# Floors under squared norms inside later operations, one unit's denominators in PSUM, and a new order, in a fused hybrid block

## The chip, the cores and the metric

One Trainium2 chip, one NeuronCore. The program is a single launch over the whole input. The metric is the device time of the launch in microseconds; the kernel before takes 792.27 us (median of 3 runs, 791.22 to 794.27). Engines are named as the profile names them: PE (TensorE matmul), PEld (its weight loads), DVE (VectorE), ACT (ScalarE), POOL (GpSimd), SP (SyncE, which issues most DMAs).

## What is computed

An input of 8 sequences x 512 tokens x 128 features, float32, goes through four residual layers: a delta-rule attention, a mixture of experts, a chunked linear attention, and the same mixture of experts again.

```python
x = L0_attn_a_x                                   # (8, 512, 128)
x = x + attn_a(layernorm(x), Wq, Wk, Wv, Wb, Wo, conv_q, conv_k, conv_v, o_norm_w)
x = x + ffn(layernorm(x), Wg, W1, W2)
x = x + attn_b(layernorm(x), Wq, Wk, Wv, Wo, bo)
x = x + ffn(layernorm(x), Wg, W1, W2)

# attn_a, 16 heads of 8: q, k, v = silu(short causal conv, 4 taps, of x @ W.T)
n = sqrt(sum(q * q));  q = q / max(n, 1e-6)       # the same for k
v_new = (v_t - k_t @ S) * sigmoid(x @ Wb.T)       # one token after the other
S = S + outer(k_t, v_new);  o_t = (q_t * 8 ** -0.5) @ S
o = o * rsqrt(mean(o * o) + 1e-6) * o_norm_w      # then @ Wo.T

# attn_b, 16 heads of 8: phi = elu + 1, causal in chunks of 128
out = (A @ v + phi_q @ S) / (rowsum(A) + phi_q @ z + 1e-5)

# ffn: 8 experts, the best 2 by x @ Wg, weights renormalised, relu, 128 -> 256 -> 128
```

## The kernel before

The 512 tokens are cut in 8 **units** of 64 tokens (of all 8 sequences, so 512 rows each). A unit passes through these parts, whose names appear in the profile's tiles:

- `prepare(c)` (tiles ending in `_a`): loads x, normalises it, transposes it on PE, projects it. For units 0 to 3 the convolution's four taps are folded into the weights (`wc`, made by `weights_of_taps` and kept in the storage of experts 5 to 7, `resident[5..7]`), so q, k and v take 4 matmuls each (`s_pp_a`); for units 4 to 7 DVE applies the taps. ACT applies silu (`y_a`). The results go to DRAM (`scr`) and come back with heads on partitions (`qk`, `vv`).
- Squared norms (`nrm`): for some units by PE over the feature partitions (`norms_of`, `over_heads`, through DRAM as `scn`), for units in `NEAR_NORMS` (5, 6, 7) and for unit 0's keys by ACT and DVE after the round trip (`near_norms`). Both end with a floor of 1e-12 under the squared norm, on POOL in the first, on DVE in the second. `back` then takes the root of the keys' norms (`ri`, in a PSUM bank, `s_near_a` in the profile), inverts it, and builds the factors `W` of four tokens at a time (`substituted`).
- `recurring`: the delta rule, four tokens a step, 16 steps a unit, 128 in all, one after the other. A step is four DVE operations (`pj`, `factors`, `terms`, `st`) and copies on ACT (`values`, `beside`). POOL multiplies states by queries (`po`); for units 0 to 2 PE sums them (`s_po`).
- `ending`: corrects the outputs, normalises them (`s_rms`), where the query's squared norm stands in place of dividing the query, and sends them through DRAM (`sco`) to `oT`.
- `layers` / `of_rows`: output projection (`s_po_a`), then `moe` under the name f, `linear_attention` under b, and `moe` under g. Unit 7 is done in two halves. `moe` routes (`y_pl`: logits, first and second choice by `first_of_largest`, their weights by `relative`), spreads the combined weights through DRAM (`scw`) over all partitions, and `all_experts` runs every expert on rows scaled by their weight: POOL scales (`wt_xsT`), PE multiplies (`s_ph`), ACT applies relu (`hT`), PE multiplies again (`y_py`). For units 0 and 7 expert 0's rows are scaled before a transpose instead (`TURNED`, `TURNED_IN`).
- `attend`, inside `linear_attention`: POOL forms the products of keys and values (`kv`), PE sums them causally (`s_pc_b`), DVE multiplies by the queries and reduces (`qs`, `nd`), adds 1e-5 to the denominators (`dn`), inverts them and scales. For unit 0 the sums are in SBUF (`nd`), for later units in PSUM (`pS`).
- `loading_later_weights`: SP loads the experts' weights, 3 DMAs an expert. Experts 5 to 7 wait until unit 3's projections have read the tap weights lying there.

**The order.** The program text describes parallel streams; a `Weaver` runs them once and so writes down each engine's order of instructions. Each operation has a modelled duration (the function `duration`, and additions by `weaver.took`). Of the streams whose next step can start soonest, the weaver takes the one with the largest priority: what is still behind it in the chain of work (`chains`, from four earlier passes that only plan) plus two tables of constants, `FAVOURED` by part and `OFFSETS` by stream. On the chip each engine runs its instructions in that order and waits on semaphores; the modelled durations have no other effect. Where the weaver expects PE to wait 0.6 us or more, `keep_busy` puts in matmuls on constants (line 1950, tile `busy`), 0.22 us each for seven tenths of the expected gap; they write to a free PSUM bank and compute nothing that is used.

PSUM has eight banks: five general ones (`banks`, tiles `s_...`), two long ones (`y_...`), and one for the recurrence's `factors`.

All engine calls go through one helper, so nearly all of the profile's rows carry its line, 454; they are told apart by tile.

Of the kernel before, what the change touches and what calls it, by code (L numbers as in the profile page):

```python
# [19 lines left out]
P = 128  # L20
# [17 lines left out]
TURNED = 1  # L38
# [8 lines left out]
ADDED_ON_DVE = (4,5,6,7)  # L47
NEAR_NORMS = (5,6,7)
# [5 lines left out]
TURNED_IN = (0,7)  # L54
# [13 lines left out]
PASSES = ()  # L68

FAVOURED = {  # L70
    ("b", 0.0): 1475, ("b", 1.0): -605, ("b", 2.0): 408, ("b", 3.0): -1141, ("b", 4.0): 1159, ("b", 5.0):
    -397, ("b", 6.0): -3095, ("b", 7.0): -2237, ("b", 7.5): -2071, ("beside",): 1509, ("ending",): 696,
    ("f", 0): 1839, ("f", 1): 922, ("f", 2): 673, ("f", 3): -941, ("f", 4): 1648, ("f", 5): 1050, ("f", 6):
    -1587, ("f", 7): 767, ("f", 7.5): -2892, ("g", 0.0): 1576, ("g", 1.0): 901, ("g", 2.0): 357, ("g", 3.0):
    7212, ("g", 4.0): -253, ("g", 5.0): -2424, ("g", 6.0): -246, ("g", 7.0): 1986, ("g", 7.5): -2626,
    ("outputs",): 7, ("prepare", 0): -904, ("prepare", 1): -3306, ("prepare", 2): 224, ("prepare", 3):
    -1571, ("prepare", 4): -839, ("prepare", 5): -16, ("prepare", 6): 680, ("prepare", 7): -2427, ("recur",
    0): 3219, ("recur", 1): -6342, ("recur", 2): -2844, ("recur", 3): 482, ("recur", 4): -2744, ("recur",
    5): -1405, ("recur", 6): 1064, ("recur", 7): -724, ("values",): 149, None: -1498,
# [4 lines left out]
    -5735, -5206, -179, -62, -5753, 0, -6219, -6323, 29, -6838, 1464, 2372, 2338, -2, 1277, -3446, -3136,  # L84
    2417, -3137, -2112, -3119, -3650, -311, 76, 1, 3, -3, 77, -342, -7970, 977, -20, -4091, 3665, -19, 806,
    -4343, -4621, -4648, -4379, 711, 806, -5289, 1734, 1900, 1275, 623, -5269, -420, -380, -832, -1479, 50,
    -758, -790, 125, -3620, 585, -553, 237, 2322, 2064, -5521, 501, -5381, -5928, -3498, -40, 2563, 4086,
    10628, -5495, 782, 11097, 2142, 524, -2998, -175, 1440, -9862, 334, 747, 94, -5047, -6796, 307, 308,
    -1787, -402, -3506, -63, -187, 265, -2927, -6059, -6411, -6618, 0, -4528, -6371, -6553, -6091, -5056,
    263, -538, -1107, -6503, -6983, -6, -6510, -36, -961, -967, 294, 389, -6742, -8230, -142, -7747, -8737,  # L90
    -7250, -7254, -7665, -422, 1935, 282, -996, -6683, -9031, 177, 1221, 466, 360, -7342, 552, -8817, -42,
    -7371, 101, 1699, 247, 245, 186, -7410, 57, 713, -5151, 127, -91, -80, -5933, 56, -6006, -6402, 412,
    -6116, -445, 35, 2434, -4925, -4928, -4874, -938, 1079, 406, -7960, 775, 519, -186, -183, -6551, -7752,
    -7695, -8113, 429, 2079, 1870, 73, 72, 717, 130, -428, -37, 347, 2267, 385, -69, 3340, -640, -367, 165,
    -831, -1483, 0, 486, -5539, -200, -199, -399, -34, 2547, -7582, -106, -2671, 11037, 1388, 1383, 1120,
    -962, 17, -1270, -6162, -175, -5673, 211, 50, -7246, -2444, -7484, -2599, -386, 24, -1456, -1295, -1542,
    449, 95, 3319, -2490, -5181, -17, 250, 1245, 968, 926, -3459, -1, -51, -7241, -6288, -40, -5786, 456, 0,
    2, -7292, 471, -361, -79, -6239, 1121, 209, 228, 171, -490, -335, -1339, -4313, -4533, -173, -162,
    -1885, -4676, -5235, -6460, -342, -6601, -6575, 266, 235, 4646, 4647, 78, -899, -7489, 388, -348, 4,
    2051, 1488, -3366, -170, -1594, -5834, -4738, -590, -6081, 2703, 771, 806, 2101, -1052, -4471, -334,  # L100
    10046, 384, -6869, -6546, 10224, -8058, 323, -1252, 463, 8950, 0, -8361, 1480, -113, -361, -8416, -9767,
    -47, -200, -9523, 27, -8517, -60, 66, -8349, -229, -9575, -9613, 177, 0, -516, 2087, 1808, 1102, -3472,
    -3462, -3444, -261, -48, -604, -199, 8924, -1499, -2626, 0, -5333, -68, 0, -3882, -1964, 1388, 1387,
    -3692, -5022, -5065, -555, 136, 6558, 1420, 1897, 1801, 9994, 299, 277, 324, -41, 8082, 391, 7156, 7157,
    -5841, -322, -1273, -5351, 627, 9366, -2233, -2747, 1391, 674, -7825, -11438, -30, 775, 2023, 1821,
    -1660, -376, -7698, 679, -3112, 1424, -5849, 0, -55, 151, -899, 680, -7529, -8147, 148, 896, 1077, 914,
    339, 108, 425, -1456, -5019, -1472, -477, 2580, -4207, -3854, -4163, -8696, -1145, -4645, -48, -435,
    -49, -441, -2007, 528, -6603, 2721, 2590, 71, 790, 1764, 678, -1104, -11, -8403, -631, -307, -17, 8979,
    -26, 111, 125, -3643, 387, 709, -7661, -6188, -1529, 52, -267, -2256, -1638, -163, -7464, -7718, -7716,
    -1060, 1984, -7251, 341, -416, 74, 246, 826, 0, -1331, 114, -9262, 817, -794, -1132, -4670, 22, 677,  # L110
    -1102, -247, -991, 5324, 1460, 7056, -68, 22, -4777, -5911, -267, -245, 0, -5384, 611, 1441, -3227,
    -3228, 7000, -4910, -4927, 8594, 7076, 656, 8970, 534, 0, -414, -452, 8696, 199, -1793, 526, 7399,
    -2385, -2142, -2082, 703, 601, -344, 673, 889, 675, -225, 700, 0, 1159, -2605, -52, 1613, 16, -121, 10,
    3158, 128, 131, -45, -73, 1613, -6492, -6728, -6847, 1627, -162, 2762, 283, 57, -585, 605, 1, -6681,
    -6644, -7468, 1614, -1785, -6492, 3296, -2793, 740, 1374, 1438, -5170, -5140, 909, 2571, -5016, 298,
    -5165, -4644, -50, -42, -4475, 2, 294, -85, -2740, -6839, 226, 1693, -57, 3901, -15, 128, 27, -353,
    1777, -988, 548, -1117, 51, -5550, -5713, 147, 12, -34, -4251, 1589, 1915, 47, -3918, 1053, 111, -9287,
    183, -73, -1509, -1272, -1576, 1611, -436, 1, 5846, -1241, -112, 1631, -1205, 1597, 150, -2745, -3535,
    2377, 2411, 1644, 1676, -1215, 1575, -4452, 8420, 702, -792, 816, 406, 430, 763, 8525, 846, -158, 8634,
    8574, 7499, -111, 1400, 1450, 1002, 8654, -2038, 769, 762, 607, 2855, 6551, -97, -90, -87, 5399, 647,  # L120
    -2965, 11537, -1025, 26, 1690, -128, 1901, -2876, -579, -1637, -1629, 2367, 1239, 1591, 19, 1583, 1724,
    11913, 9792, -979, -5647, 234, 2469, -6345, 305, -458, 202, 495, 2179, 331, -2292, 9691, 1045, 6, 9790,
    35, -5846, 323, 577, 1291, 9691, -58, -97, 118, -5, -4, 615, -5886, 76, -98, -106, -3895, 613, 2012,
    -4473, 833, 614, 2011, -59, -171, -3273, -3336, -3353, -3, -4885, 1032, 10012, 4, 9990, -8535, 13, -26,
    -426, 9852, -8409, 100, -8705, 1140, -1782, -3, -354, -197, -1938, -335, 9717, -197, 9802, 2602, -4020,
    6594, -4069, 2798, 3058, 2, -79, -78, 391, 1966, 1709, 200, 8716, 1885, 10615, 11418, 3662, 9797, 2272,
    1035, 2099, 0, 1824, 10195, 9823, 10532, 9755, 10009, 1333, 1142, -251, 8119, 297, 296, 41, 749, 4723,
    747, 1875, 2107, 724, -124, 453, 7278, 3607, 3799, 273, 3441, 3113, -3692, -398, -3768, -334, -3765,
    -3766, -582, -412, 9876, -382, 1211, 10712, -1001, 93, -1201, 9799, -302, 9584, 9796, 780, 9701, -580,
    1068, 9799, -828, -878, 2215, 2732, -4744, 3104, 2677, 2684, 2623, 238, -387, -153, 2284, -614, 2072,  # L130
    231, 2027, -4996, -71, 30, 457, -4797, 384, -249, 4030, 2190, -5523, 4173, 1217, 3083, 1929, -714, 605,
    676, -732, -321, -57, 3956, 733, 11526, -7059, -800, 1502, 239, -723, -808, -318, -541, 8037, -8544, 15,
    -4952, -5089, -5252, -4993, 2029, -304, -831, -5698, -69, -6182, -350, -409, 2461, 257, -282, -7155,
    -5747, 0, -11360, 2325, 2107, 2122, 386, -5700, -3106, -1352, 0, 0, -1541, 372, -1538, -3081, -1573,
    -1435, -66, 3013, -2727, -4066, -895, -131, -4357, 2917, -4077, -498, 0, -3157, -80, -404, -3201, -3374,
    0, 1576, 1292, 11286, -3695, -3696, 11437, 2265, 10445, 11425, 0, 3814, -3061, -6147, -44, -59, 400,
    8019, -14, -1979, -5119, 523, -2588, 5587, 523, -3171, -3206, -10, -3214, -2710, -659, 484, -3058,
    -1775, -2867, 1019, -1081, -5, 52, 3008, 2887, 58, -126, 9551, 2973, 9821, 1860, 1206, 1067, -225, -506,
    1503, 155, -134, -730, 2292, 869, 1769, 471, 90, 1950, 3546, 1948, 683, 11408, 1149, -376, -1944, 1011,
# [1869 lines left out]
```

## Time and profile before

| | us |
|---|---|
| median of 3 runs (lowest, highest) | 792.27 (791.22, 794.27) |
| the profiled execution, its own time | 790.81 |
| its span, from the first to the last instruction | 789.1 |
| DVE: the recurrence's four operations, 128 times each | 61.4 + 58.4 + 53.7 + 53.4 |
| POOL: the two groups of 55 expert rows, 512 wide | 69.5 + 69.2 |
| PE: 195 fillers | 52.7 |
| PE: the wait for the first weights | 3.54 |
| mean TensorE clock granted | 0.991 |

A row of the profile's groups reads: line, engine, operation, written tile <- read tiles, shape, count, then the busy time and the mean of one in ns, then the idle time of that engine just before these instructions and what ended it. A matmul of float32 is recorded as two instructions, so a 512-wide one, with 592 ns recorded for each half, is two rows that overlap; in a dense stretch the next one starts 0.86 us later. The fillers are bfloat16 and are one row each.

### The profile page before, as it was taken

How to read it: one execution, taken by the hardware profiler on the slowest of the kernel's cores; microseconds unless marked ns; L12 is line 12 of the kernel's file. 1: busy time of each engine (PE TensorE's matmuls, PEld its weight loads, DVE VectorE, ACT ScalarE, POOL GpSimd, SP SyncE). 2: the span in 40 equal slices, each digit the busy share in tenths (PEclk: the TensorE clock that was granted, in tenths of full speed). 3: DMA queues.
4: the chain of work that ended last, by engine and by line, in shares of the span. 5: the costliest groups of instructions: out<-in, count | busy, mean ns of one | idle time of the engine just before them, and what ended most of it. 6: DMA issues, size and time to landing. Idle time of an engine off the chain costs nothing.

```text
span 789.1 us, 11578 instructions
## 1 busy us (share of the span) xinstructions
PE 758.7 (96%) x3383; PEld 384.7 (49%) x3383; DVE 560.8 (71%) x1429; ACT 504.7 (64%) x1388; POOL 446.0 (57%) x609
## 2 busy tenths in 40 slices
PE   8888899997999999999999999999999999999997
PEld 4344454553435434544444435453444456644475
DVE  1689898978997698899999799798557145342310
ACT  5765767688877865678676875773664445643352
POOL 1244447659586495775586664877736606735331
PEclk9999899998999999999999999999999999999999
DMA  1451426105233311214132132232112211321121
GB/s 46 118 133 42 123 63 183 45 23 148 69 97 80 98 56 55 81 55 126 54 111 96 34 102 78 82 106 67 42 41 81 60 28 48 108 69 44 37 60 34
DMA packets 82392, 59.67 MB, mean 76 GB/s; under 512 B 48152, under 2 KB 64152, under 8 KB 82328
## 3 DMA queue, kind: packets, MB, share of 16 engines
q1 hardware_dynamic: 81608, 58.64, 25.8%
q8 instruction: 27, 0.44, 0.2%
q10 hardware_dynamic: 720, 0.28, 0.2%
q14 instruction: 37, 0.30, 0.1%
HBM read 46.52 MB, written 12.39 MB: 75 GB/s over the span
## 4 chain that ended last, share of the span: by engine, by line
PE 78%; DVE 11%; ACT 6%; issue 2%; DMA 2%; POOL 1%; SPq 0%; DVEq 0%; ACTq 0%; POOLq 0%
PE s_ph_f L454 14%; PE y_py_f L454 13%; PE s_ph_g L454 13%; PE y_py_g L454 12%; PE s_pc_b L454 5%; PE s_pp_a L454 4%; PE s_pp_b L454 2%; PE busy L1950 2%; PE s_pu_b L454 2%; DVE st L454 2%; PE s_pS_b L454 2%; DVE W L454 1%; ACT squares L454 1%; DVE pj L454 1%; DVE terms L454 1%
## 5 line engine op out<-in xcount | busy, mean ns | idle before, releaser
L454 ACT ACTIVATE hT_g<-s_ph_g 128x512 f32<-128x512 f32 (+1 forms) x144 | 79.0, 552 | 95.5 <-PE s_ph_g L454 94.5
L454 PE MATMUL y_py_f<-hT_f,resident 128*128 128x512 f32 (+1 forms) x288 | 134.3, 555 | 0.3 <-ACT hT_f L454 0.2
L454 PE MATMUL s_ph_f<-wt_xsT_f,resident 128*128 128x512 f32 (+1 forms) x288 | 132.1, 554 | 1.9 <-POOL wt_xsT_f L454 1.1
L454 PE MATMUL y_py_g<-hT_g,resident 128*128 128x512 f32 (+1 forms) x288 | 133.3, 553 | 0.3
L454 PE MATMUL s_ph_g<-wt_xsT_g,resident 128*128 128x512 f32 (+1 forms) x288 | 131.0, 553 | 0.3 <-POOL wt_xsT_g L454 0.2
L454 ACT ACTIVATE hT_f<-s_ph_f 128x512 f32<-128x512 f32 (+1 forms) x144 | 78.7, 550 | 50.9 <-PE s_ph_f L454 49.4
L454 POOL TENSOR_TENSOR wt_xsT_g<-wt_xsT_g,xn_xnT_g 128x512 f32<-128x512 f32 (+1 forms) x69 | 79.0, 1166 | 37.0 <-DMA wt_xsT_g<-scw_g 26.7
L454 POOL TENSOR_TENSOR po<-st,kq 128x256 f32<-128x256 f32 x128 | 93.8, 763 | 3.3 <-DVE st L454 2.7
L454 POOL TENSOR_TENSOR kv_b<-ph_b,v 128x1152 f32<-128x1152 f32 x32 | 69.2, 2176 | 39.8 <-ACT v L454 27.1
L454 POOL TENSOR_TENSOR wt_xsT_f<-wt_xsT_f,xn_xnT_f 128x512 f32<-128x512 f32 (+1 forms) x69 | 79.4, 1168 | 17.5 <-DMA wt_xsT_f<-scw_f 17.4
L454 DVE TENSOR_TENSOR qs_b<-s_pc_b,ph_b 128x360 f32<-128x360 f32 (+1 forms) x96 | 50.4, 551 | 46.2 <-PE s_pc_b L454 45.5
L454 PEld LDWEIGHTS y_py_f<-hT_f,resident 128*128 128x128 f32 x288 | 50.6, 190 | 47.2 <-issue 40.4
L454 PEld LDWEIGHTS s_ph_f<-wt_xsT_f,resident 128*128 128x128 f32 x288 | 50.4, 190 | 47.4 <-issue 31.6
L454 PEld LDWEIGHTS y_py_g<-hT_g,resident 128*128 128x128 f32 x288 | 50.9, 190 | 44.1 <-issue 35.6
L454 PEld LDWEIGHTS s_ph_g<-wt_xsT_g,resident 128*128 128x128 f32 x288 | 50.9, 190 | 43.7 <-issue 32.0
L454 DVE TENSOR_REDUCE st<-terms 128x64 f32<-128x320 f32 x128 | 61.4, 480 | 12.3 <-ACT terms L454 6.0
L454 DVE TENSOR_REDUCE factors<-pj 128x32 f32<-128x288 f32 x128 | 58.4, 456 | 6.2 <-ACT factors L454 2.5
L1950 PE MATMUL busy<-ones 128*128 128x512 bf16 x195 | 52.7, 411 | 9.5 <-ACT o L454 3.4
L454 DVE TENSOR_TENSOR pj<-st,factors 128x256 f32<-128x256 f32 x128 | 53.4, 417 | 4.7 <-ACT factors L454 1.8
L454 DVE TENSOR_TENSOR terms<-factors,kt 128x256 f32<-128x256 f32 x128 | 53.7, 419 | 4.2 <-ACT vn L454 1.1
L454 ACT COPY terms<-st 128x64 f32<-128x64 f32 x128 | 39.6, 309 | 25.0 <-DVE st L454 23.8
L454 POOL TENSOR_TENSOR pq<-y_a,y_a 128x128 f32<-128x128 f32 x32 | 21.1, 685 | 46.2 <-ACT squares L454 23.1
(270 smaller groups left out, 1336.1 us busy)
## 6 DMA issues: line engine op xcount, KB each, us to landing
wt_xsT_f<-scw_f SPq DMA_DIRECT2D x55, 256.0 KB
wt_xsT_g<-scw_g SPq DMA_DIRECT2D x55, 256.0 KB
scr<-y_a SPq DMA_DIRECT2D x24, 256.0 KB
qk<-scr SPq DMA_DIRECT2D x16, 256.0 KB
x_a<-in_x_dram SPq DMA_DIRECT2D x16, 128.0 KB
vv<-scr SPq DMA_DIRECT2D x8, 256.0 KB
sco<-on SPq DMA_DIRECT2D x8, 256.0 KB
oT<-sco SPq DMA_DIRECT2D x8, 256.0 KB
```

Source lines behind the costliest of these rows:

```text
L454: r = call(*args, **kw)
L1950: nc.tensor.matmul(pt, ones, ones.unsqueeze(1).to_broadcast([P, 4, P]), start=True, stop=True)
```

## The change

It has five parts that touch instructions, one that touches the model, and one that replaces the order.

1. *Floors.* POOL keeps its floor under the keys' squared norms only; the queries' floor moves into the ending, where the squares are scaled beforehand so that one operation takes the maximum and adds. `near_norms` loses its floor; for unit 0 and units 5 to 7 a floor of 2e-6 under the doubled root, on the PSUM tile, takes its place.
2. *Denominators.* For unit 0, `dn` lies in a general PSUM bank.
3. *Tap weights.* They move from `resident[5..7]` to the storage of `kv`. The loads of experts 5 to 7 wait for nothing; the first unit's linear attention waits for the tap matmuls of unit 3.
4. *Routing.* The two choices' weights (`relative`) are worked out as soon as the second maximum is known, beside the search for its place.
5. Several options are added and set to empty (`STATES_ON_PE`, `KEYS_ON_POOL`, `QUERIES_ON_POOL`); `TURNED` becomes a table with the same content.
6. *Durations in the model.* POOL's power, copies and products, ACT with a bias or a scale from memory, and a few additions.
7. *Order.* The chains get one further pass (`PASSES`: how long before the end each step must start), and both tables of constants are new (1005 offsets before, 1023 after).

```diff
-TURNED = 1
+TURNED = {"f0": 1, "g0": 1, "f7": 1, "g7": 1}
...
+STATES_ON_PE = ()
+KEYS_ON_POOL = ()
+BURST = NE - 3
...
-TURNED_IN = (0,7)
...
-PASSES = ()
+PASSES = ((1, 0.0, {}),)
...
-        more = (0.19 if "bias" in kw else 0.0) + (0.0 if isinstance(scale, float) else 0.08)
+        more = (0.1 if "bias" in kw else 0.0) + (0.0 if isinstance(scale, float) else 0.06)
...
     if key == "POOL" and ALU.pow in args:
-        return key, 1.05, 0.1
+        return key, 0.4 + n * 0.16, 0.1
     if key == "POOL":
-        return key, 0.2 + n * (1.72e-3 if n > 512 else 2.0e-3), 0.1
+        if op == "tensor_copy":
+            return key, 0.16 + n * 1.3e-3, 0.1
+        return key, 0.18 + n * (1.73e-3 if n > 512 else 2.15e-3), 0.1
...
-    wc = [resident[NE - 3 + s].rearrange("p (k d) -> p k d", k=4) for s in range(3)]
+    kv_ = const.tile([P, 2, NH, V1, HD], F32, name="kv")
+    taps = kv_.rearrange("p w h e d -> p (w h e d)")[:, 0 : 12 * D].rearrange("p (s k d) -> p s k d", s=3, k=4)
+    wc = [taps[:, s] for s in range(3)]
...
-    kvs = held_in(1, [P, 2, NH, V1, HD], "kv")
+    kvs = Slots(weaver, None, None, "kv", 1, [kv_])
...
         for e in range(NE):
-            if TAPS_ON_PE and e >= NE - 3:
-                yield fired("projected", TAPS_ON_PE - 1, e - (NE - 3))
             for to, by in [(slice(0, NF), f_w1[e])] + [
...
                 sp.dma_start(resident[e][:, to], by)
+                if e >= BURST and to.stop < 2 * NF:
+                    weaver.moves(-LANDS)
...
         pool.tensor_tensor(rs, rs, mhalf[:, 0:nb], ALU.pow)
-        weaver.took("POOL", 0.8)
...
             yield from over_heads(flat, nrm[:, s], s)
-            yield "POOL" if CLAMP_ON_POOL else "DVE"
-            (pool if CLAMP_ON_POOL else dve).tensor_scalar(
-                nrm[:, s], nrm[:, s], ATT_A_EPS * ATT_A_EPS, None, ALU.max
-            )
+            if s:
+                yield "POOL"
+                pool.tensor_scalar(nrm[:, s], nrm[:, s], ATT_A_EPS * ATT_A_EPS, None, ALU.max)
...
-            yield "DVE"
-            dve.tensor_scalar(nrm[:, s], nrm[:, s], ATT_A_EPS * ATT_A_EPS, None, ALU.max)
             fire("norms", c, s)
...
             act.activation(ri, nrm[:, 1], AF.Sqrt, scale=4.0)
+            if c == 0 or c in NEAR_NORMS:
+                yield "DVE"
+                dve.tensor_scalar(ri, ri, 2.0 * ATT_A_EPS, None, ALU.max)
...
-        act.activation(so, o, AF.Square)
+        act.activation(so, o, AF.Square, scale=(ATT_A_EPS * HD * HD) ** -0.5)
...
-        dve.scalar_tensor_tensor(rms, nrm[:, 0], ATT_A_EPS * HD * HD, rms, ALU.mult, ALU.add)
+        dve.scalar_tensor_tensor(rms, nrm[:, 0], ATT_A_EPS * ATT_A_EPS, rms, ALU.max, ALU.add)
         yield "ACT" if c in ROOTS_SOON else "sqrt"
-        act.activation(rms, rms, AF.Sqrt, scale=1.0 / HD)
+        act.activation(rms, rms, AF.Sqrt, scale=ATT_A_EPS * HD)
...
+        def first_of_largest(p, k):
+            m = near(nb) if k else row(f"m{k}")
+            yield "DVE"
+            dve.tensor_reduce(m, p, AX.X, ALU.max)
+            if k:
+                scales["weights"] = spawn(relative(m1, m))
...
-        m2 = yield from first_of_largest(lg2, 1)
...
-        yield from relative()
...
+        yield from first_of_largest(lg2, 1)
+        yield scales["weights"]
...
+        if c == 0:
+            yield from all_of([fired("projected", TAPS_ON_PE - 1, s) for s in range(3)])
         kv = yield from kvs.take(n)
...
-        dn = yield from dns.take(n)
-        if c > 0:
+        if c == 0:
+            of_dn = yield from banks.take(f"dn_{n}")
+            dn = of_dn[:, 0 : 2 * NH].rearrange("p (i h) -> p i h", i=2)
+        else:
+            dn = yield from dns.take(n)
             yield turned
```

The tables `FAVOURED` and `OFFSETS` are replaced whole and are not shown; the largest offset goes from 12802 to 5424.

## The prediction

> **What bounds the kernel now.** I began with the page: busy times and the forty slices.
>
> ```profile
> PE 758.7 (96%) x3383; PEld 384.7 (49%) x3383; DVE 560.8 (71%) x1429; ACT 504.7 (64%) x1388; POOL 446.0 (57%) x609
> ...
> PE   8888899997999999999999999999999999999997
> ...
> DVE  1689898978997698899999799798557145342310
> ...
> PEclk9999899998999999999999999999999999999999
> ```
>
> TensorE is the bound: three quarters of the slices have it at nine tenths. But 195 of its instructions compute nothing; they are the fillers of line 1950 that stand where the layout expected a gap. So I asked for the engines' busy time by stretch, and then for the fillers alone in the same stretches (columns: stretch, length, PE, PEld, DVE, ACT, POOL busy, clock, DMA share, GB/s).
>
> ```profile
> 0.00:100.00 100.00, 86.74 (x412) 44.28 (x413) 69.56 (x180) 65.97 (x195) 38.18 (x84) 0.97 0.35 94
> 100.00:200.00 100.00, 90.92 (x442) 50.39 (x441) 86.86 (x215) 75.26 (x222) 64.13 (x96) 0.97 0.33 91
> ...
> 300.00:400.00 100.00, 99.80 (x456) 48.49 (x456) 90.96 (x220) 69.72 (x189) 64.06 (x81) 1.00 0.28 85
> ```
>
> ```profile
> 0.00:100.00 100.00, 33.66 (x131) 13.46 (x132) 0.97 0.35 94
> 100.00:200.00 100.00, 14.70 (x51) 5.25 (x49) 0.97 0.33 91
> ...
> 560.00:789.10 229.10, 4.00 (x14) 1.37 (x14) 1.00 0.20 56
> ```
>
> In the first 200 us PE is busy 86.74 + 90.92 = 177.66 us, of which 33.66 + 14.70 = 48.36 is filler: useful work is 129.3, so 70.7 us are lost while the first units come through their recurrences. After 200 us it is busy 758.73 - 177.66 = 581.1, less 0.38 and 4.00 of filler, so 576.7 useful of 589.1: 12.4 lost, 4.3 of them after the last matmul (it ends at 784.84, the span at 789.1). The useful work, 706 us, is the same after the change. **The whole case is therefore the 83 us lost, and almost all of it is the filling of the pipeline.** What can be had there is limited by VectorE too: from 24 us to 100 it is busy 66.2 of 76, then 86.9 of 100.
>
> Next I looked for a place in the filling that is a mistake of the order and not a lack of work, in the timeline (start, length, engine; in brackets the idle time before and what ended it).
>
> ```profile
> 179.00 2.53 POOL L454 TENSOR_TENSOR wt_xsT_f<-wt_xsT_f,xn_xnT_f 128x512 f32<-128x512 f32 x2
> ...
> 183.94 0.43 PE L454 MATMUL s_pn_a<-sq,heads 128*32 128x128 f32 x8
> ...
> 186.63 5.07 PE L1950 MATMUL busy<-ones 128*128 128x512 bf16 x12 [2.27 <-ACT v L454]
> ...
> 191.54 2.74 PE L454 MATMUL s_ph_f<-wt_xsT_f,resident 128*128 128x512 f32 x6
> ```
>
> Unit 1's first two scaled expert inputs are written by 181.5, yet its first expert matmul starts at 191.54. Queued ahead of it are eight small matmuls (0.43) and twelve fillers, and the fillers wait for ACT's v before they run. That is 191.54 - 181.5 - 0.43 = 9.6 us lost. The clock granted from 172 to 192 is 0.83 on average: the twelve fillers take 0.42 us each, against 0.22 for the twenty at 60.59 (4.48 us).
>
> **The change, part by part.** *Floors.* Five of nine POOL floors go (row 128x64, 381 ns): 5 x 0.38 = 1.9 us of an engine that is 57% busy. Seven DVE floors of 541 ns mean go, 3.8 us, and four come on a PSUM tile. The trace has no such form; the nearest rows are these.
>
> ```profile
> L454 DVE TENSOR_SCALAR nrm<-nrm x7: 186/370/1220, 25.1 to 478.7; 128x64 f32<-128x64 f32 x7
> ...
> L454 DVE TENSOR_SCALAR dn_b<-s_pS_b x14: 183/191/192, 306.7 to 738.1; 128x32 f32<-128x32 f32 x14
> L454 DVE TENSOR_SCALAR dn_b<-nd_b x2: 248/437/626, 216.7 to 240.8; 128x32 f32<-128x32 f32 x2
> ```
>
> Minimum, median, maximum in ns: on SBUF the same operation spreads from 186 to 1220, with PSUM as its source from 183 to 192. I price the new floor at 0.2 (bounds 0.19 and 1.22), so DVE gains 3.8 - 0.8 = 3.0 us; at the other bound it loses 4.9 - 3.8 = 1.1. On the path only unit 0's counts: it loses 0.20 at 25.09 and gets 0.2 back between ACT's root and the reciprocal, so 0 (bounds 0 and +1.0). The others lie after 275 us, beside a PE that is busy 99.80 of 100; without that cover the three together would cost 0.6. The floor and the scale folded into the ending add no instruction: 0. Had these saved what they remove, all of it on the path, the gain would be 3.0.
>
> [...]
>
> *Denominators of unit 0 in PSUM.* Two attention pairs, three operations each, by the rows: (0.437 - 0.191) + (0.463 - 0.424) + 0 = 0.29 us each, 0.6 us of DVE at 217 to 242 us, where PE is busy 97.6 of 100: 0. They hold one of five general banks for about 1 us; if a matmul waits for it, 2 x 1 us is the bound.
>
> *Routing weights beside the second choice.* For unit 0's first experts the chain from m2 (112.99) to the combined weights (118.14) is 5.15 us: four operations for the one-hot, then two, tanh on ACT, two more, then the product and the sum. The two strands may now overlap. DVE still does every one of them, at 0.5 us pitch between steps of the recurrence; what goes is the wait around tanh, from 116.08 to 116.39, and half the alternation. I take 1.0 us (bounds 0 and 2), once; later routings lie beside a full PE.
>
> *Tap weights in kv's tile.* Experts 5 to 7 no longer wait for unit 3's projections. Nine loads, now issued from 116 to 146 us among unit 0's row loads, come earlier. Each holds SP's queue about 0.45 us; all nine ahead of a recurrence's loads would cost 4.1, but SP's queue is empty for 10 us from 66. Unit 3's 24 half-matmuls at 106.35 to 117.65 may move behind unit 0's experts; they end before the weights they stand beside (118.14), so taking them away gains 0 to 0.6: 0. In exchange POOL's first kv waits for unit 3's last tap matmul. POOL would hold the pos and row scalings queued behind it, and PE waits for both; it starts at 186.98, 69 us after that matmul, so 0 unless unit 3 slips that far.
>
> *The order.* The code shows how a layout's gap becomes fillers: 0.7 of it, at 0.22 us. Twelve fillers at 186.63 mean 12 x 0.22 / 0.7 = 3.8 us expected, where 9.6 were lost. In all, 195 x 0.22 / 0.7 = 61.3 us were expected; 83.1 less 3.5 before the first matmul and 4.3 after the last makes 75.3. So about 14 us stand between the plan and the chip. Three corrected durations go to the rows: the power on POOL was 1.85 and is 1.04 (row 1039 ns), the expert row 1.22 and is 1.28 (row 1280), the 64-wide copy 0.33 and is 0.24 (row 238). One goes away from them: an ACT square with a bias was 0.49 and is 0.40, while the rows show 402 ns and a start every 0.52, since an accumulator read follows. A right plan takes back what the plan did not know; I take the one place seen, 9.6 - 3.8 = 5.8 us, with bounds of 14 to the good and, since every priority is new, 10 to the bad (below).
>
> **Sum.** Against the profiled execution's own 790.81 (span 789.1 and 1.7 around it): 790.81 - 5.8 - 1.0 = 784.0. That execution is 1.46 under the median of 792.27, so I forecast **785.5**, itself between 776 (14 and 2 off) and 789.
>
> **Rivals.** *Preparation ahead of the recurrence.* Unit 1's preparing takes DVE ten us (0.55, 0.20, 0.22, 0.68, 1.03, then eleven rows of 0.42 to 0.83, from 65 to 78); from 71.6 to 79.4 the recurrence stands still for it. If the new priorities put one more unit's preparation ahead of unit 1's recurrence, its experts start 10 us later, with nothing else for PE: 790.81 + 10 + 1.46 = **802**. For it: every priority is replaced, and the filling has DVE at 87%. Against it: such a delay needs no unit after it to have work ready. It decides from about 5 us of delay on, beyond what the plan's corrections give back.
>
> *The filling is set by the round trips.* If unit 0's path (projection, transposing through DRAM, 38 us of recurrence, DRAM again to 102) fixes the filling whatever the order, the floors and the rest do nothing to the end and the time is **791.5**. For it: the fillers at 95.64 wait beside a trip through DRAM that no order removes. Against it: the 9.6 us at 182 lie on no such trip.
>
> **Chances.** The forecast 0.52, preparation first 0.37, no effect 0.11. What a measurement can tell from no change is 0.5%, 4 us: faster means under 788.3, slower over 796.2. So 0.52, 0.11 and 0.37. The range takes both sides: 773 to 804 leaves out about one in ten at either end (over 19 us recovered from the median, more than the plan's 14 and the routing's 2; a delay past 12).
>
> **What would show it.** Right: fillers in the first 200 us fall from 48 us to near 43, unit 1's first expert matmul comes at 185 or before, PE stays at 99% from 200 on, useful PE at 706. Wrong: unit 0's first expert matmul later than 122.7, unit 1's later than 195, kv waiting for a tap matmul, or PE gaps after 200. DVE's total should fall by about 3 to 4 us whatever the time does.

## The result, and the profile after

The changed kernel takes **796.36 us** (median of 10 runs, 795.67 to 797.62) against 791.25 us for the kernel before (10 runs, 789.65 to 795.6): ratio **1.0061**, 95% interval 1.0045 to 1.0076. It is slower by 5.1 us, where the forecast was 785.5 with a chance of 0.37 for slower; the time lies in the forecast's range, on the other side of no change. The profiled execution took 797.55 us with a span of 795.8 (790.81 and 789.1 before).

The page's busy times:

```profile
PE 758.9 (95%) x3366; PEld 386.0 (49%) x3366; DVE 568.9 (71%) x1426; ACT 506.3 (64%) x1391; POOL 445.2 (56%) x604
```

PE is busy for as long as before (758.9 against 758.7), in a span that is 6.7 us longer, and DVE, which was to lose 3 to 4 us, has gained 8.1. Two of the stretches (stretch, length, busy time of PE, PEld, DVE, ACT, POOL, granted clock, DMA share, GB/s):

```profile
100.00:200.00 100.00, 85.68 (x415) 48.39 (x412) 88.50 (x214) 77.87 (x230) 63.65 (x97) 0.94 0.31 84
300.00:400.00 100.00, 97.49 (x417) 46.08 (x417) 90.90 (x227) 71.62 (x194) 68.57 (x92) 1.00 0.27 76
```

From 100 to 200 us PE was busy 90.92 us with 14.70 of filler; now it is 85.68 with 10.39 (42 fillers, line 2011 now). In 300 to 400 it was at 99.80 and is at 97.49. These are the two places where the time went: PE stands still for 5.2 us more in the one and 2.3 more in the other. The first in detail, in PE's timeline (start, length, instructions, tiles; in brackets the idle time before and what ended it):

```profile
186.51 3.78 PE L453 MATMUL s_po<-po,ident 128*128 128x128 f32 x16 [4.68 <-POOL po L453]
...
195.45 3.75 PE L453 MATMUL s_ph_f<-wt_xsT_f,resident 128*128 128x512 f32 x4 [2.92 <-ACT v L453]
```

Unit 1's first expert matmul (`s_ph_f`) comes at 195.45, 3.9 us **later** than before (191.54), not at 185 or earlier. Ahead of it PE idles 4.68, 0.75 and 2.92 us with no filler, and what runs after a wait runs at half pace: the sixteen transposes `s_po` take 3.78 us, the four expert matmuls 3.75. Stretches of the same time (stretch, length, PE busy, granted clock, DMA share, GB/s) say why:

```profile
184.00:190.00 6.00, 3.49 (x16) 0.50 0.66 210
...
194.00:200.00 6.00, 4.55 (x6) 0.50 0.00 0
```

The clock is 0.83 in the microsecond from 183 and 0.76 in that from 190, 0.95 from 193 and 0.64 from 200: it is half from 183.7 to 190.5 and from 193.9 to 200.7, and the useful matmuls in these two stretches are busy for 9.1 us, half of it lost. Before, there was one such stretch here, 184.5 to 191.4, and only fillers ran in it.

### The profile page after: what moved, and what is told of

The parts are those of the page before. It is cut to its first block, busy times and chain, and to the rows that moved or that the text cites. A ratio compares the mean times of both kernels' runs of the same rounds, so it can differ in the third digit from the quotient of the medians.

```text
span 795.8 us, 11543 instructions
## 1 busy us (share of the span) xinstructions
PE 758.9 (95%) x3366; PEld 386.0 (49%) x3366; DVE 568.9 (71%) x1426; ACT 506.3 (64%) x1391; POOL 445.2 (56%) x604
## 4 chain that ended last, share of the span: by engine, by line
PE 71%; DVE 17%; ACT 5%; POOL 4%; issue 3%; DMA 0%; DVEq 0%; ACTq 0%; POOLq 0%
PE y_py_g L453 13%; PE s_ph_g L453 12%; PE y_py_f L453 11%; PE s_ph_f L453 11%; PE s_pp_a L453 4%; PE s_pc_b L453 4%; DVE st L453 3%; DVE factors L453 2%; DVE terms L453 2%; DVE pj L453 2%; PE s_pp_b L453 2%; PE s_pu_b L453 2%; ACT squares L453 2%; PE s_pS_b L453 1%; PE s_po L453 1%
## 5 line engine op out<-in xcount | busy, mean ns | idle before, releaser
L453 PE MATMUL y_py_g<-hT_g,resident 128*128 128x512 f32 (+1 forms) x288 | 131.5, 550 | 0.0
L453 POOL TENSOR_TENSOR kv<-ph_b,v 128x1152 f32<-128x1152 f32 x32 | 69.3, 2176 | 35.0 <-DVE ph_b L453 20.5
L453 POOL COPY st<-st 128x64 f32<-128x64 f32 x31 | 7.4, 239 | 71.9 <-DVE st L453 68.7
```

The costliest lines, as they stand in the source:

```text
L453: r = call(*args, **kw)
```

## The experiments

Each experiment ran beside the kernel before on the same chip; ratios are to those runs. A number in brackets is the 95% interval.

| kernel | median us | ratio to the kernel before |
|---|---|---|
| the changed kernel | 796.36 | 1.0061 [1.0045, 1.0076] |
| edits of the instructions, old order | 790.81 | 1.0008 [0.9993, 1.0023] |
| old order, without the twelve fillers | 793.03 | 1.0028 [1.0017, 1.0039] |
| old order, kept warm | 792.28 | 1.0016 [1.0007, 1.0025] |
| old order, kept warm, experts in order of readiness | 789.78 | 0.9985 [0.9975, 0.9996] |
| new order, gaps filled | 793.92 | 1.0037 [1.0024, 1.0050] |
| old order, no sums on ScalarE | 790.01 | 0.9986 [0.9977, 0.9995] |
| new order, no sums on ScalarE | 795.16 | 1.0059 [1.0044, 1.0073] |
| new order, no sums, gaps filled | 792.53 | 1.0025 [1.0014, 1.0036] |
| new order, gaps filled, roots later | 793.06 | 1.0021 [1.0008, 1.0034] |
| new order, gaps filled, corrected output later | 793.14 | 1.0024 [1.0012, 1.0036] |
| new order, gaps filled, both moves | 791.76 | 1.0002 [0.9990, 1.0015] |

### The edits, or the order?

The first kernel is the one before with the edits and without the new order (the plan still counts the instructions that are gone, so that the order stays).

```diff
-    wc = [resident[NE - 3 + s].rearrange("p (k d) -> p k d", k=4) for s in range(3)]
+    kv_ = const.tile([P, 2, NH, V1, HD], F32, name="kv")
+    taps = kv_.rearrange("p w h e d -> p (w h e d)")[:, 0 : 12 * D].rearrange("p (s k d) -> p s k d", s=3, k=4)
+    wc = [taps[:, s] for s in range(3)]
...
+            if s:
+                pool.tensor_scalar(nrm[:, s], nrm[:, s], ATT_A_EPS * ATT_A_EPS, None, ALU.max)
...
+            if c == 0 or c in NEAR_NORMS:
+                nc.vector.tensor_scalar(ri, ri, 2.0 * ATT_A_EPS, None, ALU.max)
...
-        dve.scalar_tensor_tensor(rms, nrm[:, 0], ATT_A_EPS * HD * HD, rms, ALU.mult, ALU.add)
+        dve.scalar_tensor_tensor(rms, nrm[:, 0], ATT_A_EPS * ATT_A_EPS, rms, ALU.max, ALU.add)
```

> The kernel before, in its own order, with the instruction edits of the change: the floors out of POOL's and VectorE's norms, the floor on the PSUM tile for unit 0 and units 5 to 7, the floor and scale folded into the ending, the tap weights in kv's storage. Not in it: the new order, the new durations, the routing split, the denominators in PSUM. The theory that the order alone loses the time expects 791 +- 1.5 us, no difference to the kernel before. The theory that the edits themselves cost the 5 us (a PSUM floor on the path of unit 0, kv waiting for the taps) expects 795 to 796 and unit 0's first expert matmul later than 122.7. My forecast priced these edits at 0.

790.81 us, ratio 1.0008: no difference. The floors, the folded ending and the taps in kv's tile cost and bring nothing that can be measured, so nearly all of the 5 us are the order's. (The denominators in PSUM and the routing's two strands were not run alone.)

### The place that the forecast rested on

The forecast saw unit 1's scaled rows ready at 181.5 and the first expert matmul at 191.54, behind twelve fillers. Two kernels take those fillers away or replace them, in the old order:

```diff
-            for _ in range(n):
+            for _ in range(0 if n == 12 and weaver.clock["PE"] > 150.0 else n):
```

> The kernel before without the twelve fillers ahead of unit 1's first expert matmul, which my forecast held for the mistake of the order (9.6 us lost, 5.8 to be had). By the forecast's reading unit 1's first expert matmul comes 5 us earlier or more and the time falls by 5 to 9, to 782 to 786. By the theory that the clock is what counts, the matmul comes at 186.6, but the clock stays halved over it and the following ones, which gives half back: 788.5 to 789.5.

```diff
+            if spare_bank and 182.0 < weaver.clock["PE"] < 190.0:
+                pt = spare_bank[0].rearrange("p (a b) -> p a b", a=4)
+                count = 8 if weaver.clock["PE"] < 184.0 else 7 if weaver.clock["PE"] < 188.0 else 10
```

> The kernel before with the fillers laid out for 182 to 190 us (3, 3 and 12) replaced by 8, 7 and 10 that write into unit 1's held output bank, so that none waits for the bank of v and TensorE is kept busy where it now idles before the twelve. The clock theory expects full clock from 184 to 192 us, unit 1's first expert matmul near 187 (191.54 before), and 786 to 787 us, faster than both kernels. If unit 1's first expert matmul is set by its operands or by VectorE's later work, 790 to 791.

Both came out slower than the kernel before: 793.03 and 792.28 us. Neither forecast nor rival had this. PE's timeline without the twelve, and then kept warm:

```profile
191.41 5.49 PE L454 MATMUL s_ph_f<-wt_xsT_f,resident 128*128 128x512 f32 x6 [6.07 <-POOL wt_xsT_f L454]
```

```profile
190.41 4.24 PE L454 MATMUL s_ph_f<-wt_xsT_f,resident 128*128 128x512 f32 x6 [3.80 <-POOL wt_xsT_f L454]
```

With the fillers out of the way the first expert matmul waits 6.07 and 3.80 us for POOL's `wt_xsT_f`: the rows were not ready. POOL's timeline of the kernel before has the answer:

```profile
179.00 2.53 POOL L454 TENSOR_TENSOR wt_xsT_f<-wt_xsT_f,xn_xnT_f 128x512 f32<-128x512 f32 x2
...
182.08 1.29 POOL L454 TENSOR_TENSOR wt_xsT_f<-wt_xsT_f,xn_xnT_f 128x512 f32<-128x512 f32 x1
...
189.11 1.27 POOL L454 TENSOR_TENSOR wt_xsT_f<-wt_xsT_f,xn_xnT_f 128x512 f32<-128x512 f32 x1
```

One such instruction scales one expert's rows. The old order scales experts 1 and 3 at 179.00, expert 2 at 182.08 and expert 0 at 189.11; PE begins with expert 0. So the rows that count were ready at 190.38, not at 181.5, and the fillers cost 1.2 us of the 9.6. Taking them away lets PE idle for 6 us, the clock falls (0.50 from 191 to 196), and the six expert matmuls take 5.49 us where they took 2.74. Kept warm, they start 1.1 us earlier than before, but after the 3.80 us of waiting the clock is at half over them (0.50 from 192 to 195), and they end 0.4 us later.

The next kernel removes the true wait as well: kept warm as above, and the row that POOL scales first belongs to the expert that PE takes first.

```diff
+ORDER = {"f1": {1: 0, 3: 1, 2: 2, 0: 3}}
...
-                sp.dma_start(rows, scw[e : e + 1, 0 : nb * P].to_broadcast([P, nb * P]))
+                sp.dma_start(rows, scw[x : x + 1, 0 : nb * P].to_broadcast([P, nb * P]))
...
-            scaled[e] = xsT
+            scaled[({} if isinstance(tc, Quiet) else ORDER.get(name, {})).get(e, e)] = xsT
```

> The kernel before with the fillers of 182 to 190 us replaced by 8, 7 and 10 in the held output bank, and with unit 1's first four experts taken in the order in which POOL scales their rows (1, 3, 2, 0 as they stand now), so that TensorE's first expert matmul no longer waits for the row scaled last, at 189.1 to 190.4. My forecast took 9.6 us at this place as lost by the order of the queue, 5.8 to be had. If that is so, the first expert matmul comes at 186.6 to 187 (191.54 before) at full clock, and the time falls by 4 to 5, to 786 to 787. If what follows (VectorE's steps, the next rows) sets the pace, the time stays at 790 to 792.

```profile
187.25 1.10 PE L455 MATMUL s_ph_f<-wt_xsT_f,resident 128*128 128x512 f32 x2 [0.36 <-DVE ph_b L455]
189.54 1.98 PE L455 MATMUL s_ph_f<-wt_xsT_f,resident 128*128 128x512 f32 x4 [1.19 <-ACT narrow_nt_a L455]
```

The first expert matmul comes at 187.25, 4.3 us earlier, at full clock, and the time falls by 1.6 us (0.9985), where 4 to 5 were expected. Behind the removed wait stand 1.19 us until ACT's copy `narrow_nt_a`, and 1.49 until ACT's relu ahead of the second matmuls; these start at 193.01, only 1.1 us earlier than before (194.12). This kernel is faster than both kernels of the case.

### Gaps that no filler filled

`keep_busy` returns when no general PSUM bank is free. In the new order this is so in two planned gaps of 3.89 and 2.62 us (the plan's own arithmetic), which on the chip lie between 181 and 192. In a third, of 3.04 us and ahead of the first expert matmul, a bank is listed, but it comes free only when the gap is over. The held output bank of unit 1's experts is free until their first result, so the fillers can go there; nothing else moves.

```diff
         if gap < 0.6 or not banks.free or weaver.clock.get("PE", 0.0) < WA_LANDS:
+            if gap > 2.0 and spare_bank and not banks.free and len(unfilled) < 3:
+                unfilled.append(gap)
+                for _ in range((12, 8, 9)[len(unfilled) - 1]):
+                    nc.tensor.matmul(
+                        spare_bank[0].rearrange("p (a b) -> p a b", a=4), ones,
+                        ones.unsqueeze(1).to_broadcast([P, 4, P]), start=True, stop=True,
+                    )
             return
```

> The changed kernel with its order untouched, and 12, 8 and 9 fillers in the three stretches of 181 to 196 us where TensorE waits and the layout put none, because no general PSUM bank was free; they write into unit 1's held output bank before its first real matmul. They compute nothing that is used. The theory that the halved clock after these waits costs the time expects the granted clock to stay full from 184 to 201 us, the 16 transposes at 186.5 in 1.95 us and not 3.78, the first four expert matmuls in 1.88 and not 3.75, and 791 to 792 us in all. The rival, that unit 1 is late for lack of VectorE's and POOL's work and the clock is only a symptom, expects 796 still.

```profile
181.72 2.75 PE L2009 MATMUL y_py_f<-ones 128*128 128x512 bf16 x12
186.59 3.33 PE L453 MATMUL s_po<-po,ident 128*128 128x128 f32 x16 [2.11 <-POOL po L453]
189.71 2.30 PE L2009 MATMUL y_py_f<-ones 128*128 128x512 bf16 x8
...
195.07 1.95 PE L453 MATMUL s_ph_f<-wt_xsT_f,resident 128*128 128x512 f32 x4 [2.62 <-ACT v L453]
```

793.92 us: 2.4 less than the changed kernel, the ratio falls from 1.0061 to 1.0037; 791 to 792 us were expected. The trace has 12 and 8 fillers. The nine meant for the third gap are not in it, since the edit acts only where no bank is listed, and PE still waits 2.62 us there. The first four expert matmuls take 1.95 us and not 3.75. The clock theory holds for this part, with two misses: in the profiled execution the clock still fell once, from 187 to 191 (mean 0.57), under `s_po` (3.33 us where 1.95 were expected), and 1.0037 is left, about 3 us, of which this half clock explains at most 1.4.

### ScalarE's sums: a theory that fell

The new durations make a biased square on ACT 0.40 us long, where the rows show a start every 0.52 because a read of the accumulator follows (`ACTIVATION_READ_ACCUMULATOR`, 0.19 us each, 132 in the kernel before). Walking both orders through the plan's arithmetic with 0.12 us more for each sum lengthened the new one by 10.9 us and the old by 4.2, which would have explained the reversal. So both kernels ran without the sums:

```diff
-                squares, xt[:, j, :], AF.Square, bias=mean[:, j : j + 1], scale=float(D) ** -0.5,
-                accum_out=ss[:, j : j + 1],
+                sss[:, j : j + D], xt[:, j, :], AF.Square, bias=mean[:, j : j + 1], scale=float(D) ** -0.5,
```

> The kernel before, same order, with the 132 sums that ScalarE reads out of its accumulator left out: the means and squares write their rows into a small tile, and the first element stands for the sum, so the norms are scaled by other numbers. 132 reads, each making the pitch 0.52 us where the instruction alone takes 0.40. Theory A (the new order was laid out with 0.40 for these instructions and has no slack for the reads, the old one with 0.49) expects the kernel before to gain little, 0 to 4 us: 787 to 791. The rival (the order is worse for another reason, ScalarE's reads hurt both alike) expects the same gain here as in the changed kernel.

> The changed kernel, same order, with the same 132 sums left out. Theory A: walking the two fixed orders through the layout's own arithmetic with 0.12 us more for each sum lengthens the new order by 10.9 us and the old by 4.2, so the changed kernel should gain 6 or more, to 790 or less, and come out level with the kernel before without its sums, or ahead. The rival expects the gap of 5 us between the two to stay.

> The changed kernel without the 132 sums and with the 12, 8 and 9 fillers of the earlier run in the three stretches at 181 to 196 us. If the halved clock (2.4 us, measured) and the sums are two separate causes, the gains add: about 2 us under the changed kernel without sums. If the sums alone made TensorE wait there, the fillers now gain nothing or cost up to 1 us.

Without its sums the kernel before takes 790.01 us (0.9986) and the changed one 795.16 (1.0059): 1.2 to 1.4 us each, and the gap of 5 stays. The 10.9 us were the plan's, not the chip's. The fillers bring 2.4 us with the sums and 2.6 without, so the two are separate and the sums aren't the cause of the gap.

### The rest of the difference, in two moves

Two places remained, each read from the trace. First, POOL's queue ahead of `po` in the changed kernel, and what waits for it:

```profile
181.54 1.04 POOL L453 TENSOR_TENSOR rs_a<-rs_a,mhalf 128x4 f32<-128x4 f32 x1
...
183.42 3.04 POOL L453 TENSOR_TENSOR po<-st,kq 128x256 f32<-128x256 f32 x4
```

The root of unit 5's layer norm (`rs_a`, four instructions from 181.23 to 183.17, the power above among them), needed by ACT at 190.5, stands ahead of unit 2's `po`. `s_po` waits for `po`, ACT's copy of `o` for `s_po`, `v` stands behind that copy, and the first expert matmul takes the PSUM bank that `v` frees (its wait above reads `ACT v`). Second, DVE's timeline at 329, and PE's waits after it:

```profile
330.79 2.00 DVE L453 SCALAR_TENSOR_TENSOR oc<-vn,qk 128x128 f32<-128x128 f32 x1
```

```profile
330.47 2.18 POOL L453 TENSOR_TENSOR kv<-ph_b,v 128x1152 f32<-128x1152 f32 x1
```

```profile
337.86 0.44 PE L453 MATMUL s_pt_q_b<-ident,ph_b 128*128 128x128 f32 x2 [0.85 <-ACT xn_xnT_b L453]
...
340.70 0.84 PE L453 MATMUL s_pc_b<-kv,tri 64*64 64x360 f32 x8 [0.65 <-DVE x_a L453]
```

The corrected output `oc` takes 2.00 us here, and 0.28 at 189.58: it starts inside POOL's product `kv` (330.47 to 332.64) and ends at 332.79, when that has ended. The recurrence's step behind it comes 1.7 us late, ACT's copies wait for the step, and PE waits 0.85 and 0.65 us for what stands behind those copies.

The moves are made on the changed kernel with the gaps filled, in the list of steps that the weaver wrote down; each kernel has one of the three first lines. The second changes DVE's order and nothing else. The first changes POOL's order and, through it, the fillers, which these kernels count by the rule (seven tenths of a planned gap): with `po` planned earlier, 7 stand ahead of `s_po` and 13 behind it, where there were 12 and 8.

```diff
+MOVED = ((1586, 1631),)                  # POOL: unit 5's root behind unit 2's four po
+MOVED = ((3140, 3154), (3151, 3140))     # DVE: oc behind the recurrence step it held up
+MOVED = ((1586, 1631), (3140, 3154), (3151, 3140))
...
+    for picked, behind in MOVED:
+        moved = next(p for p in order if p[0] == picked)
+        order.remove(moved)
+        order.insert(next(n for n, p in enumerate(order) if p[0] == behind) + 1, moved)
```

> The changed kernel with the fillers of the first experiment, and one thing moved in POOL's queue: the four small operations that make unit 5's layer-norm root (1.94 us at 181.2 to 183.2) stand behind unit 2's state products po instead of ahead of them. TensorE's transposes s_po wait for po, ScalarE's copy of o waits for these, and v, whose PSUM bank the first expert matmul of unit 1 takes, stands behind that copy. Theory B (unit 1 starts late through this queue, and its lateness is carried to the end) expects s_po near 184.7 (186.59 before), unit 1's first expert matmul at 192.7 to 193.2 (195.07), and 791.5 to 792.5 us (793.9 without the move). The rival (work lost there is made up later) expects 793.5 to 794.

> The changed kernel with the fillers, and one VectorE operation moved: the corrected output oc at 330.8, which takes 2.00 us there where it takes 0.28 elsewhere, since it runs beside POOL's 2.17 us product kv, stands four operations later, behind the recurrence step that it holds up. Theory C (VectorE is held for POOL's operation, the recurrence and ScalarE's copies come 1.7 us late, TensorE waits 0.85 and 0.65 us at 337 and 340) expects oc in 0.3 to 0.8 us, both of TensorE's waits gone, and 792.2 to 792.7 us (793.9 without the move). The rival expects the waits to stay or the time to be lost elsewhere: 793.5 to 794.

> The changed kernel with the fillers and both moves. If the two causes are separate and TensorE is the bound behind both, the gains add: 790 to 791 us, level with the kernel before (790.8 to 791.4). If only one of the two counts, this run equals the better of the two.

793.06, 793.14 and 791.76 us; in ratios 1.0037 falls to 1.0021 and 1.0024 by the one and the other, and to **1.0002** by both. The gains add (0.0016 + 0.0013 against 0.0035), and the intervals of the single moves overlap that of the kernel they start from, but that of both together does not. Alone, each came out between its theory and its rival: 793.06 where 791.5 to 792.5 were expected, and 793.14 where 792.2 to 792.7 were. In the traces each does what it was to do. PE's timeline of the first kernel, then DVE's and PE's of the second:

```profile
180.17 1.67 PE L2025 MATMUL y_py_f<-ones 128*128 128x512 bf16 x7
183.03 2.05 PE L458 MATMUL s_po<-po,ident 128*128 128x128 f32 x16 [1.19 <-POOL po L458]
184.92 2.97 PE L2025 MATMUL y_py_f<-ones 128*128 128x512 bf16 x13
...
191.28 2.38 PE L458 MATMUL s_ph_f<-wt_xsT_f,resident 128*128 128x512 f32 x4 [2.92 <-ACT v L458]
```

```profile
330.27 0.43 DVE L458 SCALAR_TENSOR_TENSOR oc<-vn,qk 128x128 f32<-128x128 f32 x1
```

```profile
336.25 0.84 PE L458 MATMUL s_pc_b<-kv,tri 64*64 64x360 f32 x8 [0.24 <-DVE x_a L458]
```

`oc` takes 0.43 us; PE's first wait, ahead of `s_pt_q_b`, is gone, and the second is 0.24. With the roots later `s_po` runs at full clock (2.05 us against 3.33), and the first expert matmul comes at 191.28, 3.8 us earlier than in the filled kernel (about 2 were expected), but the clock halves over it; with both moves it comes at 192.35 at full clock.

So the 5.1 us are accounted for: fillers that found no bank and the clock behind them, 0.0024; a root in POOL's queue ahead of `po`, with the fillers that moved along and the clock, 0.0016; one DVE operation that lasted until POOL's had ended (2.00 us where 0.28 to 0.43 do), 0.0013; together 1.0061 comes down to 1.0002. How the 0.0016 divides between root, fillers and clock no run shows. All three are in the order and none is in an edited instruction. The old order has none of them: its planned gaps at this place had a bank, unit 2's `po` run from 175.70 to 179.05 and unit 5's root only at 198.25, and its `oc` took 0.28 us in seven of eight units and 0.81 in one. It has faults of its own, as the 0.9985 above shows; none of the three cures was tried in it.

## Why the prediction was wrong

- **What bounds the kernel: right.** PE is the bound and its busy time is the same. Useful PE time was to be 706 us; it is 758.9 less 46.0 of filler, 712.9, and 4.5 of the 6.9 more are the half clock in the two stretches above.
- **The failed step** is the one that gave the forecast its size: "Unit 1's first two scaled expert inputs are written by 181.5, yet its first expert matmul starts at 191.54 [...] That is 191.54 - 181.5 - 0.43 = 9.6 us lost". The two inputs were those of experts 1 and 3. A tile's name carries no expert, and I took the first two rows of that name for the first two that PE needs. Of the 9.6 us, 1.2 lay in the queue. With the true wait removed too, the place was worth 1.6 us (0.9985), not 5.8, since two waits on ACT stood right behind it. And the new order does not mend this place: the first expert matmul comes 3.9 us later in it.
- **"A right plan takes back what the plan did not know":** this inference failed too. By the plan's own arithmetic, each kernel with its own durations, the changed one is 4.3 us shorter (796.0 against 800.3); on the chip it takes 5.1 longer. The plan knows neither the clock nor that a DVE operation can take longer beside a POOL one (`oc` 2.00 us against 0.28), and it doesn't fill a gap for which no general bank is free. Nor does it see the two moves: by its arithmetic the later roots leave it at 796.0 and the later `oc` lengthens it to 796.8, while on the chip both moves together gain 0.0035. That the time still lies in the forecast's range is the range's doing: it is 31 us wide, and its upper end came from a rival.
- **Floors, folded ending, taps at nothing: right.** In the old order 1.0008. The floor on the PSUM tile was priced at 0.2 and takes 0.22 to 0.23 us; unit 0's denominators take 218, 362 and 414 ns, near the numbers taken for them (191, 345, 424). But the SBUF rows that the forecast set against PSUM's 191 ns, 248 and 626, were both taken beside a POOL operation, and don't show what PSUM alone is worth. Alone the floor took 0.19 to 0.20 us on SBUF (186 and 195 ns) and 0.22 to 0.23 on the PSUM tile (220 and 233), so it is slower there by 0.02 to 0.05 us. What PSUM saved is the spread: the other two of the four new floors ran beside a POOL operation and took 0.23 as well, where the floors on SBUF went up to 1.22.
- **DVE's total: wrong.** "DVE's total should fall by about 3 to 4 us whatever the time does"; it rose by 8.1. Eight `oc` take 7.4 us where they took 2.8, and seven `s_spare_a <- W, kq` take 7.0 where they took 3.1, with the same shapes. The row that I showed for the floor, 186 to 1220 ns on SBUF, was the same thing, and I read it as a spread: the one of 1220 ran from 275.99 to 277.21 beside a POOL product that ended at 277.16, and the two that met no POOL operation took 0.19 and 0.20 us.
- **Routing beside the second choice: about right, and of no use.** From `m2` to the combined weights it takes 4.5 us (108.55 to 113.04) and took 5.15; 1.0 was expected. Unit 0's first expert matmul came at 118.19 and not 122.68, but the unit's last transposes at 165.36 and not 164.30. What unit 0 gained was lost within 47 us.
- **The rivals.** "Preparation ahead of the recurrence" had the right sign, the right kind of cause (the new priorities make unit 1 late, its experts by 3.9 us) and a price of 10 where 5.1 came. A preparation did come forward: the power of unit 5's root runs at 181.54, before at 198.57. But the mechanism is another: not ten us of DVE's ahead of unit 1's recurrence, but 1.9 us of POOL's ahead of unit 2's `po`, and one `oc`, with the unfilled gaps and the clock as the largest part (0.0024 of 0.0059, and some of the root's). "No effect" fell.
- **The signs** chosen beforehand worked: unit 1's first expert matmul at 195.45 (wrong beyond 195) and PE at 97.49 of 100 after 300 us (99 wanted) pointed to the two places where the time was found. One sign misled: the fillers of the first 200 us fell from 48 to 43.8 us, as they should have for a right forecast, because gaps went unfilled.

## What to carry to other kernels

A tile's name in a profile can stand for several objects; before a gap ahead of a consumer is booked as a mistake of the queue, take the suspected blocker away and see whether another wait takes its place. A new order of a schedule laid out by hand or by a search must be judged on the chip: a plan that leaves out the clock and what a DVE operation takes beside a POOL one (2.00 us against 0.28) was wrong by 9 us between two orders (4.3 shorter against 5.1 longer), more than all the edits together. Where a filler keeps PE warm, give it a bank that is always free, since a gap that can't be filled costs the gap and, as here, may cost half clock over the useful work behind it (the four expert matmuls took 3.75 us, and 1.95 with two of the gaps filled).

## What the runs showed of the hardware

**The clock and short waits.** In the profiles of the kernel before and the changed one, a stretch at half clock lasted 3.41 or 6.83 us up to the last matmul; without the twelve fillers it was 10.2 us in all between 183 and 200. In each of the two profiles all of them begin and end on one grid of 3.41 us: in the changed kernel at 67.61, 71.02, 183.66, 190.49, 193.90 and 200.73, in the kernel before at 92.38, 99.21, 184.54 and 191.37. PE need not stand still for as long: in the 3.4 us ahead of nine stretches in six profiles it was busy for 1.12 to 1.80 us.

| 3.4 us up to the fall, from | PE busy, us |
|---|---|
| before, 88.97 and 181.13 | 1.12, 1.69 |
| changed, 64.19, 180.25 and 190.49 | 1.80, 1.59, 1.31 |
| edits in the old order, 293.90 | 1.13 |
| new order, gaps filled, 183.70 | 1.31 |
| old order, kept warm, 188.30 | 1.29 |
| new order, roots later, 189.28 | 1.40 |

From 20 us on, in the first two of these profiles, a full clock stayed after one step of the grid with 1.44 us of PE busy (before, from 51.42) and after every one with 2.07 or more, and fell after those with 1.59, 1.69 and 1.80. So a wait of one length halves the clock or not. With the roots later and with both moves PE waits 2.92 us for `v` at the same place, with half clock behind it in the one and full clock in the other. The three microseconds from 193 (stretch, length, PE busy, granted clock, DMA share, GB/s) in the one and the other:

```profile
193.00:196.00 3.00, 3.00 (x4) 0.50 0.00 0
```

```profile
193.00:196.00 3.00, 3.00 (x8) 1.00 0.02 5
```

**A DVE operation that lasted through several of POOL's.** The profiled execution of the edits in the old order took 794.47 us, its median is 790.81. In it one DVE operation (`s_spare_a <- W, kq`, a mean of 0.45 us in the kernel before) took 4.80, while POOL ended one `wt_xsT_g` and ran four `po` and another `wt_xsT_g` without a pause, and PE later waited 2.66 us for what stands behind it on DVE:

```profile
283.45 4.80 DVE L454 TENSOR_TENSOR s_spare_a<-W,kq 128x256 f32<-128x256 f32 x1
```

```profile
283.93 2.80 POOL L454 TENSOR_TENSOR po<-st,kq 128x256 f32<-128x256 f32 x4
286.67 1.29 POOL L454 TENSOR_TENSOR wt_xsT_g<-wt_xsT_g,xn_xnT_g 128x512 f32<-128x512 f32 x1
```

It ended at 288.25, 0.3 us after the last of these. `oc` beside `kv` is like it: it ended at 332.79, 0.15 us after `kv`. What keeps DVE in such an operation no run shows.
